# A two-layer graph attention kernel: adjacency requests and layer-1 pieces in other places of the issue order

## The chip, the cores and the metric

The kernel runs on one core of one Trainium2 chip. The metric is the device time of one execution in microseconds (us), lower is better. The kernel before was run three times: 2113.18, 2113.61 and 2120.83 us, with a median of 2113.61. One more execution was recorded by the profiler; it took 2115.05 us.

Names of engines: PE is TensorE, DVE is VectorE, ACT is ScalarE, POOL is GpSimd, SP is SyncE (here it only issues DMAs). L1029 is line 1029 of the kernel before.

## What is computed

There are 4096 nodes with 512 features (`x`) and a 4096 x 4096 symmetric 0/1 adjacency `adj`. Layer 0 is graph attention with 8 heads of width 64 over the whole adjacency, layer 1 is an attention inside 32 graphs of 128 consecutive nodes. Each layer adds its input and normalizes the rows.

```python
def layer0(X, A, W, a_self, a_neigh, b):          # 8 heads of 64
    feats = einsum('nf,hfo->hno', X, W)
    s_self = einsum('hno,ho->hn', feats, a_self)
    s_neigh = einsum('hno,ho->hn', feats, a_neigh)
    dense = s_self[:, :, None] + s_neigh[:, None, :]
    dense = where(dense > 0, dense, 0.2 * dense) * A[None]
    attn = softmax(dense, axis=-1)                 # not masked: non-neighbours count as exp(0)
    out = einsum('hij,hjo->hio', attn, feats) + b[:, None, :]
    return relu(out.transpose(1, 0, 2).reshape(N, 512))
def layer1(x, b, edge, ptr, Wq, bq, Wk, bk, Wv, bv):
    a = where(same_graph, (x @ Wq.T + bq) @ (x @ Wk.T + bk).T / sqrt(512), 0)
    s = (a + b + edge) * where(same_graph, 1, -1e6)
    return (softmax(s) * same_graph) @ (x @ Wv.T + bv)
x = layernorm(x + layer0(x, adj, ...))
return layernorm(x + layer1(x, adj, adj, ...))
```

## The kernel before

**Layer 0** goes over the adjacency in 4 passes r = 0 to 3, one for each pair of heads (`main_pass`, L1263). A pass has 4 chunks c of 1024 destination nodes, and a chunk has 32 row blocks j of 128 source nodes. These are taken in cycles of 8 (`wide=8`, passes 0 to 2) or 4 (pass 3). For a cycle the code writes out: the DMA loads of scaled features (f_s, g_s); for each j and head a tile q on DVE (L1310, 128 x 1024: the larger of a row p_row and a scalar, times the transposed adjacency tile `at`) and its 0/1 mark on ACT (L1319) or DVE (L1315); the matmuls accf (L1330, from `at`); the matmuls acc (L1347, from q); every 8 blocks the matmuls dens (L1361, from the marks).

**A^T tiles.** `bring` (L1074) makes the tile `at` for a step (r, c, j). In pass 0 it takes adjacency rows in fp8 (`a_b`, asked for by `load_adjacency`, L569, on POOL's DMA queue, which converts from fp32; 3 buffers), transposes them on PE (L1088), copies them to fp32 on ACT (L1092) and also writes them to DRAM as at_d (L1093, POOL's queue). In later passes it loads at_d on SP's queue (L1078). A cycle brings the tiles of the next one; the list `follow` (L1299) says which. There are 6 buffers of `at`, and 6 more in passes 0 to 2.

**Set-up** (L578 to L793) goes over 8 blocks k of 512 nodes. A block loads x rows (SP), transposes them (`turn_rows`, L635), computes scores on PE (L644) which ACT copies to st (L652), the exponentials from st (PE L658, then ACT and DVE), and features of four tiles u (L715). `scaled_features` scales a tile on DVE (gst, L729, 2 buffers) and on ACT and DVE (fst, L737 and L738, 2 buffers) and writes both to DRAM as g_d (256 KB) and f_d (512 KB) on POOL's queue (L750). The rows of exponentials go to DRAM as pu_d (L702) and, turned, into pu_all by a copy on DVE (L708). After the last block, S_col is made on DVE from 32 small matmuls (L785 to L793). Three adjacency requests, for row blocks 0, 4 and 8 of chunk 0, stand in the set-up at the ends of blocks 4, 5 and 6 (L778). Two rows p_row of 512 KB (broadcast from pu_d), for the first chunk, are loaded on SP's queue.

**End of a chunk.** `sums_to_rows` (L1127) adds accf and acc to ys and copies dens to dcs; its pieces, the item E below, transpose dcs (L1178, 4 times) and ys (L1201, 8 times) on PE, reduce the counts on DVE (`parts` L1181, `rd` L1191 to L1194) and scale ys to hst (L1202). In pass 3 the result and the earlier heads (hp_l, loaded from DRAM) are joined to x1b (L1123, 8 operations for a block of 512 rows) and normalized: statistics L524 and L525 on DVE, rstd on POOL (L527, L528), the result on DVE (L530).

**Layer 1** goes over 8 blocks of 512 nodes. A block is a generator (`layer_1`, L931) whose pieces are: transposes of x1b (L937, two pieces), zT (L957, then ACT's copy L964, two pieces), then scores in one piece (L984, the minimum on DVE L993, the exponentials ns on ACT L1009, `values(0)` L1029, transposes of ns L1058 with ACT's copy pT_f L1060, `values(1)`), `rows_out((0, 1))` (L1043, y_f on DVE L1045, layer norm, output), `values(2)` and `values(3)`, `rows_out((2, 3))`. `values` is four L1029 matmuls and one addition v_t on DVE (L1037).

**The order of the work.** PE's instructions run in the order in which the code writes them out. In pass 3, from chunk 1 on, pieces of E and of layer 1 are woven into layer 0's cycles by a written plan: `PLAN` (L1235) has for each cycle of four row blocks (group) two strings; the first is run ahead of the cycle's acc matmuls and the second behind them (`pieces`, L1276, called at L1340 and L1358). A letter advances a generator by one piece: E the chunk's end, b and a two blocks of layer 1, R the join of a second block. What is left after pass 3 is run by one last string (L1428), the tail. The other engines' instructions are put in order by a scheduler; each engine and each DMA queue keeps its order. PE's small results go to PSUM tiles from `misc` (L548), which takes its pools in turn; after pass 0 these hold three buffers (ps_misc 1, ps_misc2 2).

Of the kernel before, what the change touches and what calls it, by code (L numbers as in the profile page):

```python
# [404 lines left out]
def adjacency_streamed_path(  # L405
# [32 lines left out]
    NT = N // P  # L438
    FC = F // P
    PR = H // 2  # L440
# [6 lines left out]
    NCH = N // C  # L447
# [100 lines left out]
    def misc(shape, dtype=F32):  # L548

        banks.append(banks.pop(0))  # L550
        return banks[-1].tile(shape, dtype, name="ps_m")
# [4 lines left out]
    def ring(name, pool, n):  # L556

        if name not in more:
            return pool
        k = turns[name] % (n + more[name][1])  # L560
        turns[name] += 1
        return pool if k < n else more[name][0]
# [6 lines left out]
    def load_adjacency(c, j):  # L569

        a_b = pools["adj"].tile([P, CT, 4 * P], FP8, name="a_b8")
        a_bs[c, j] = a_b
        return nc.gpsimd.dma_start(
            a_b, adj[ts(c, C), j * P : (j + 4) * P].rearrange("(t p) n -> p t n", p=P)
        )


    with tc.tile_pool(name="setup1", bufs=1, side="right") as one, tc.tile_pool(  # L578
# [11 lines left out]
        def load_rows(k):  # L590
            xts[k] = []
            for u in range(4):
                xt = xtp.tile([P, F], F32, name="xt_f")
                nc.sync.dma_start(xt, x[ts(4 * k + u, P), :])
                xts[k].append(xt)
# [34 lines left out]
        def turn_rows(k):  # L630
            xT = xTs[k] = two.tile([P, FC, 4, P], F32, name="xT_f")
            for c in range(FC):
                pt = pss.tile([P, 4, P], F32, name="ps_set")
                for u in range(4):
                    nc.tensor.transpose(pt[:, u, :], xts[k][u][:, ts(c, P)], ident)  # L635
                nc.scalar.activation(
                    xT[:, c], pt, AF.Identity, accum_out=xs[:, c, k : k + 1]
                )

        def scores(k):  # L640

            ps = pss.tile([P, 4 * P], F32, name="ps_set")
            for c in range(FC):
                nc.tensor.matmul(  # L644
                    ps[32 * c : 32 * c + 32, :],
                    wa[:, c, :],
                    xTs[k][:, c].rearrange("p u n -> p (u n)"),
                    start=True,
                    stop=True,
                )  # L650
            st = sts[k] = one.tile([P, 4 * P], F32, name="st")
            nc.scalar.copy(st, ps)  # L652
# [51 lines left out]
        def columns_of_exponentials(k):  # L704
            pc = pss.tile([P, 4, 2 * H], F32, name="ps_set")
            for u in range(4):
                nc.tensor.transpose(pc[:, u, :], rows[k][:, ts(u, P)], ident[: 2 * H, : 2 * H])
            nc.vector.tensor_copy(  # L708
                pu_all[:, 4 * k : 4 * k + 4].rearrange("p u k h -> p u (k h)"), pc
            )  # L710

        def features(k, u):
            pf = pss.tile([P, H * FH], F32, name="ps_set")
            for c in range(FC):
                nc.tensor.matmul(  # L715
                    pf,
                    tile_j(xTs[k][:, c].rearrange("p u n -> p (u n)"), u),
                    w_sb[:, c, :],
                    start=(c == 0),
                    stop=(c == FC - 1),  # L720
                )
            fb = three.tile([P, H, FH], F32, name="fb")
            nc.vector.tensor_add(fb.rearrange("p h o -> p (h o)"), pf, b_row)
            return fb

        def scaled_features(k, u, fb):
            j = 4 * k + u
            gst = two.tile([P, PR, 2, FH], F32, name="gst")
            nc.vector.tensor_tensor(  # L729
                gst.rearrange("p r h o -> p (r h) o"),  # L730
                fb,
                e_all[:, j, 1, :, None].to_broadcast([P, H, FH]),
                OP.mult,
            )
            fst = two.tile([P, PR, 2, FP], F32R, name="fst")
            fr = fb.rearrange("p (r h) o -> p r (h o)", h=2)
            nc.scalar.activation(fst[:, :, 0, :], fr, AF.Copy, scale=-1.0)  # L737
            nc.vector.scalar_tensor_tensor(  # L738
                fst[:, :, 1, :],
                fr,  # L740
                -1.0,
                fst[:, :, 0, :].bitcast(F32),
                op0=OP.mult,
                op1=OP.subtract,
            )
            for dst, n, src in (
                (g_d, FP, gst.rearrange("p r h o -> p r (h o)")),
                (f_d, 2 * FP, fst.rearrange("p r s n -> p r (s n)").bitcast(F32)),
            ):
                nc.gpsimd.dma_start(dst[:, k, :, ts(u, n)].rearrange("r p n -> p r n"), src)  # L750

        turn_rows(0)
        for k in range(NB):
            if k + 1 < NB:
                load_rows(k + 1)
            fbs = [features(k, 0)]
            if k == 0:
                fbs.append(features(k, 1))
                scores(0)
            else:  # L760
                exponentials(k)
            if k + 1 < NB:
                turn_rows(k + 1)
            if k == 0:
                exponentials(0)
            scaled_features(k, 0, fbs[0])
            if k:
                fbs.append(features(k, 1))
                columns_of_exponentials(k - 1)
            scaled_features(k, 1, fbs[1])  # L770
            fbs.append(features(k, 2))
            scaled_features(k, 2, fbs[2])
            if k + 1 < NB:
                scores(k + 1)
            rows_of_exponentials(k)
            fbs.append(features(k, 3))
            scaled_features(k, 3, fbs[3])
            if k in (4, 5, 6):  # L778
                tc.keep_in_program_order(load_adjacency(0, 4 * (k - 4)))
        xsum = one.tile([P, FC], F32, name="xsum")  # L780
        nc.vector.tensor_reduce(xsum, xs, AX.X, OP.add)
        pS = pss.tile([P, PR], F32, name="ps_set")
# [291 lines left out]
    def bring(r, c, j):  # L1074

        if r:
            at = ats[r, c, j] = ring("at", atp, 6).tile([P, C], F32R, name="at")
            nc.sync.dma_start(at.bitcast(F32), at_d[c, j])  # L1078
            return
        if j % 2:  # L1080
            return
        if j % 4 == 0 and (c, j) not in a_bs:
            load_adjacency(c, j)
        pairs = a_bs[c, j - j % 4].rearrange("p t n -> p (t n)").bitcast(BF16)
        pairs = pairs.rearrange("p (t k n) -> p t k n", t=CT, k=2)[:, :, j % 4 // 2, :]
        pt = misc([P, CT, P], BF16)
        for t in range(CT):
            nc.tensor.transpose(pt[:, t, :], pairs[:, t, :], ident_b)  # L1088
        both = pt.rearrange("p t n -> p (t n)").bitcast(FP8).rearrange("p (n k) -> p n k", k=2)
        for k in range(2):  # L1090
            at = ats[r, c, j + k] = ring("at", atp, 6).tile([P, C], F32R, name="at")
            nc.scalar.copy(at, both[:, :, k])  # L1092
            nc.gpsimd.dma_start(at_d[c, j + k], at.bitcast(F32))  # L1093
# [138 lines left out]

    PLAN = [("bE", ""), ("bb", ""), ("b", "a"), ("Ra", "a"), ("a", "b"), ("ba", "b")]  # L1235
    PLANS = PLAN + [("ab", ""), ("aaba", "")], PLAN + [("a", ""), ("aa", "a")]
    plan = {"b": None}

    def run_plan(todo):
        for k in todo:  # L1240
            gen = ends[0] if k == "E" else plan[k]
            if gen is not None:
                next(gen)
            if k == "E":
                ends.pop(0)
# [15 lines left out]
    steps = [(r, c, j) for r in range(PR) for c in range(NCH) for j in range(NT)]  # L1261

    def main_pass(r, ae=None, wide=4):  # L1263

        for c in range(NCH):
# [19 lines left out]
            for j0 in range(0, NT, wide):  # L1285
# [10 lines left out]
                if at_step == 0:  # L1296
# [2 lines left out]
                follow = [  # L1299
                    x  # L1300
                    for x in steps[at_step + wide : at_step + 2 * wide]
                    if x[0] == r or 0 < r < x[0] and (x[0] < PR - 1 or x[2] < 4)
                ]
                qs = {}
                for j in cycle:
# [99 lines left out]
        banks.remove(psx)  # L1405
    first_pass.close()
    banks.extend([ctx.enter_context(tc.tile_pool(name="ps_misc2", bufs=2, space=PSUM))] * 2)
    for x_ in steps[NT * NCH : NT * NCH + 8]:
        bring(*x_)
    with tc.tile_pool(name="wl1", bufs=1, side="right") as wp:  # L1410
        work.append(weights_of_layer_1(keep, wp))
        work.append(kind_of_graphs(wp))
# [2 lines left out]
        for gen in work:  # L1415
            for _ in gen:
                pass
        work.clear()
    main_pass(2, wide=8)
    more.clear()  # L1420
    wide_passes.close()
    with tc.tile_pool(name="lp", bufs=2) as lp, tc.tile_pool(
        name="lp1", bufs=1
    ) as lp1, tc.tile_pool(name="lp2", bufs=2) as lp2:
        pools.update(lp=lp, lp1=lp1, lp2=lp2)
        main_pass(3)
        plan["K"] = kind_of_inputs(lp1)
        run_plan("bEbbbbbaaRaaKKbbababaababbbb")  # L1428


@with_exitstack
# [50 lines left out]
```

## Time and profile before

| what | value |
| --- | --- |
| median of 3 runs | 2113.61 us |
| the profiled execution | 2115.05 us |
| span of its instructions | 2113.0 us |
| mean granted TensorE clock | 0.989 of full speed |
| PE busy | 2059.4 us (97%) |
| DVE busy | 1660.3 us (79%) |
| ACT busy | 1533.8 us (73%) |
| POOL busy | 243.1 us (12%) |
| q, L1310 on DVE | 1024 of 1278 ns |
| acc, L1347 on PE | 8192, 902.7 us |
| accf, L1330 on PE | 2048, 495.3 us |

The span runs from the first to the last instruction, and the execution's time is 2.05 us longer. Busy time of an engine is the time in which one of its instructions runs; loads of weights run beside the matmuls and are listed apart. Lines of a timeline give start, duration, engine, line, operation, its operands, how often it comes in a row, and in brackets the idle time before it with what ended it.

### The profile page before, as it was taken

The page shows a single profiled execution, that of the slowest core. Times are in us where ns is not written, and L with a number is a line of the kernel's source. Part 1 is how long each engine was busy: PE and PEld are TensorE (multiplying, and loading weights), DVE is VectorE, ACT ScalarE, POOL GpSimd, SP SyncE. Part 2 cuts the span into 40 slices and gives each one's busy share as a digit, 9 for nine tenths or more (in the row PEclk, how much of TensorE's full clock was granted, in tenths as well). Part 3 has the DMA queues.
Part 4 walks back from the last instruction along what each step waited for, and adds up shares of the span by engine and source line. Part 5 has one row for each costly group of instructions (what it writes and reads, how often), then busy time and mean ns, then how long its engine had stood idle before and what let it go on. Part 6 is the DMA issues. An engine that isn't in the chain of part 4 may idle for free. (4 is left out here: it accounts for less than half of the span.)

```text
span 2113.0 us, 38133 instructions
## 1 busy us (share of the span) xinstructions
PE 2059.4 (97%) x15012; PEld 1016.1 (48%) x15012; DVE 1660.3 (79%) x2032; ACT 1533.8 (73%) x1818; POOL 243.1 (12%) x391
## 2 busy tenths in 40 slices
PE   8998999999999999999999999999999999999997
PEld 4545555455545444445445444544444445445443
DVE  5556887878789998787999999999974884786744
ACT  3327898888868889787889989998884567468320
POOL 2343222222100000000000000000210110210110
PEclk9998999999999999999999999999999999999999
DMA  8999999999879999887999999989964674665211
GB/s 246 278 215 249 276 290 258 296 256 296 267 270 342 326 366 357 273 311 254 330 319 339 306 349 325 327 304 351 307 210 144 225 250 158 207 239 165 70 48 42
DMA packets 207881, 551.28 MB, mean 261 GB/s; under 512 B 25292, under 2 KB 66252, under 8 KB 207692
## 3 DMA queue, kind: packets, MB, share of 16 engines
q1 hardware_dynamic: 140748, 425.79, 58.0%
q0 software_dynamic: 62784, 121.91, 23.0%
q8 instruction: 120, 1.97, 0.4%
q10 hardware_dynamic: 4160, 1.05, 0.2%
q14 instruction: 69, 0.57, 0.1%
HBM read 491.79 MB, written 107.22 MB: 283 GB/s over the span
## 5 line engine op out<-in xcount | busy, mean ns | idle before, releaser
L1310 DVE SCALAR_TENSOR_TENSOR q<-p_row,d_all,at 128x1024 f32<-128x1024 f32 x1024 | 1242.1, 1278 | 181.4 <-PE acc L1347 147.9
L1319 ACT ACTIVATE mark<-q,nb_all 128x1024 fp8e4<-128x1024 f32 x896 | 993.2, 1144 | 217.6 <-DVE q L1310 202.0
L1347 PE MATMUL acc<-q,g_s 128*32 128x512 f32 x8192 | 902.7, 594 | 2.9 <-DVE q L1310 2.5
L1347 PEld LDWEIGHTS acc<-q,g_s 128*32 128x32 f32 x8192 | 264.9, 110 | 594.8 <-issue 534.0
L1330 PE MATMUL accf<-at,f_s 128*128 128x512 f32 x2048 | 495.3, 398 | 5.1 <-DMA at<-at_d 4.3
L1330 PEld LDWEIGHTS accf<-at,f_s 128*128 128x128 f32 x2048 | 380.7, 189 | 115.5 <-issue 25.9
L1107 ACT ACTIVATE ck<-ck,neg_half_f 128x1024 f32<-128x1024 f32 x128 | 145.9, 1140 | 21.8 <-DMA ck<-in_adj_dram 21.5
L1108 ACT ACTIVATE ck<-ck,neg_quarter 128x1024 f32<-128x1024 f32 x128 | 146.3, 1143 | 1.9
L1092 ACT CAST at<-ps_m 128x1024 fp32r<-128x1024 fp8e4 x128 | 120.1, 1023 | 10.8 <-issue 5.9
L1029 PE MATMUL ps_m<-wvT,x1T 128*128 128x512 f32 x256 | 119.3, 615 | 6.8 <-DVE y_f L1045 6.8
L1361 PE MATMUL dens<-mark,e_b 128*6 128x512 fp8e4 x2048 | 124.3, 379 | 0.7 <-ACT mark L1319 0.7
L715 PE MATMUL ps_set<-w_sb_f,xT_f 128*128 128x512 f32 x256 | 115.4, 599 | 0.0
L957 PE MATMUL ps_m<-x1T,M_sb 128*128 128x512 f32 x256 | 113.1, 596 | 1.2 <-ACT x1T L938 1.2
L1212 POOL DMA_DIRECT2D hs_d<-hst x12 | 10.7, 895 | 847.4 <-DVE hst L1202 753.4
L1315 DVE TENSOR_SCALAR mark<-q,d_all 128x1024 fp8e4<-128x1024 f32 x128 | 95.8, 749 | 4.8
L737 ACT ACTIVATE fst<-fb 128x512 fp32r<-128x512 f32 x32 | 20.3, 634 | 101.0 <-DMA f_d<-fst 80.4
L1361 PEld LDWEIGHTS <-e_b 128*6 128x6 bf16 x2048 | 52.8, 86 | 79.8 <-issue 36.6
L1093 POOL DMA_DIRECT2D at_d<-at x128 | 69.4, 542 | 172.4 <-ACT at L1092 105.0
L1029 PEld LDWEIGHTS ps_m<-wvT,x1T 128*128 128x128 f32 x256 | 49.8, 198 | 65.4 <-issue 55.1
L957 PEld LDWEIGHTS ps_m<-x1T,M_sb 128*128 128x128 f32 x256 | 48.0, 190 | 62.6 <-issue 59.2
L1037 DVE TENSOR_TENSOR v_t<-ps_m,bv_row 128x512 f32<-128x512 f32 x32 | 21.9, 684 | 69.4 <-PE ps_m L1029 69.4
L715 PEld LDWEIGHTS ps_set<-w_sb_f,xT_f 128*128 128x128 f32 x256 | 48.8, 198 | 49.0 <-issue 48.7
(172 smaller groups left out, 1128.4 us busy)
## 6 DMA issues: line engine op xcount, KB each, us to landing
at<-at_d SPq DMA_DIRECT2D x384, 512.0 KB, 6.3
ck<-in_adj_dram SPq DMA_DIRECT2D x128, 512.0 KB, 5.5
f_s<-f_d SPq DMA_DIRECT2D x128, 512.0 KB, 7.3
at_d<-at POOLq DMA_DIRECT2D x128, 512.0 KB, 14.9
g_s<-g_d SPq DMA_DIRECT2D x128, 256.0 KB, 5.8
f_d<-fst POOLq DMA_DIRECT2D x32, 512.0 KB, 7.3
p_row<-pu_d SPq DMA_DIRECT2D x32, 512.0 KB, 7.4
a_b<-in_adj_dram POOLq DMA_DIRECT2D x32, 512.0 KB, 16.3
```

The source lines that it names most:

```text
L715: nc.tensor.matmul(pf, tile_j(xTs[k][:, c].rearrange("p u n -> p (u n)"), u), w_sb[:, c, :], start=(c == 0), stop=(c == FC - 1),)
L957: nc.tensor.matmul(pz, L1["M"][:, f, ts(c, P)], x1T[:, f, :], start=(f == 0), stop=(f == FC - 1),)
L1029: nc.tensor.matmul(pv, x1T[:, f, ts(u, P)], L1["wvT"][:, f, :], start=(f == 0), stop=(f == FC - 1),)
L1092: nc.scalar.copy(at, both[:, :, k])
L1107: tc.keep_in_program_order(nc.scalar.activation(ck, ck, AF.Square, bias=neg_half))
L1108: nc.scalar.activation(ck, ck, AF.Abs, bias=neg_quarter, accum_out=binp[:, k : k + 1])
L1310: nc.vector.scalar_tensor_tensor(q, p_row[h], d_j, ats[r, c, j].bitcast(F32), op0=OP.max, op1=OP.mult)
L1315: nc.vector.tensor_scalar(mark, q, d_j, None, op0=OP.is_gt, saturate=False)
L1319: nc.scalar.activation(mark, q, AF.Sigmoid, bias=nb_all[:, j, hh : hh + 1], scale=BIG, saturate=False,)
L1330: nc.tensor.matmul(accf[:, s, :], f_s[j // 4][:, j % 4, w, :], ats[r, c, j][:, ts(s, HB)], start=(j == 0 and w == 0), stop=(j == NT - 1 an ...
L1347: nc.tensor.matmul(acc[o : o + 32, s, :], g_s[j // 4][:, j % 4, h, o % FH : o % FH + 32], qs[j, h][:, ts(s, HB)], start=(j == 0), stop=(j ...
L1361: nc.tensor.matmul(dens[lo : lo + 6, :], e_b[:, j, 2 * r + h, :], marks[j, h][:, ts(s, HB)], start=(j == 0), stop=(j == NT - 1),)
```

## The change

It has three parts.

1. The transposed tiles for the first cycle of pass 1 (8 loads on SP's queue) are asked for in the last cycle of pass 0 by `follow`, and no more by a loop of their own between the two passes.
2. The three adjacency requests of the set-up stand at the ends of blocks 3, 4 and 5, no more of blocks 4, 5 and 6.
3. In pass 3, the first two groups of a chunk's plan are ("E", "b") and ("b", "b"), no more ("bE", "") and ("bb", ""). So E is ahead of the acc matmuls of group 0 as before, one piece of layer 1 moves from ahead of E to behind acc, and of group 1's two pieces one moves behind acc. In the tail the first three letters are bbE, no more bEb.

```diff
-            if k in (4, 5, 6):
-                tc.keep_in_program_order(load_adjacency(0, 4 * (k - 4)))
+            if k in (3, 4, 5):
+                tc.keep_in_program_order(load_adjacency(0, 4 * (k - 3)))
...
-    PLAN = [("bE", ""), ("bb", ""), ("b", "a"), ("Ra", "a"), ("a", "b"), ("ba", "b")]
+    PLAN = [("E", "b"), ("b", "b"), ("b", "a"), ("Ra", "a"), ("a", "b"), ("ba", "b")]
     PLANS = PLAN + [("ab", ""), ("aaba", "")], PLAN + [("a", ""), ("aa", "a")]
...
                 follow = [
                     x
                     for x in steps[at_step + wide : at_step + 2 * wide]
-                    if x[0] == r or 0 < r < x[0] and (x[0] < PR - 1 or x[2] < 4)
+                    if x[0] == r or x[0] < PR - 1 or x[2] < 4
                 ]
...
     banks.extend([ctx.enter_context(tc.tile_pool(name="ps_misc2", bufs=2, space=PSUM))] * 2)
-    for x_ in steps[NT * NCH : NT * NCH + 8]:
-        bring(*x_)
...
-        run_plan("bEbbbbbaaRaaKKbbababaababbbb")
+        run_plan("bbEbbbbaaRaaKKbbababaababbbb")
```

## The prediction

> **What bounds the kernel now.** I read the page's busy shares and slices first.
>
> ```profile
> PE 2059.4 (97%) x15012; PEld 1016.1 (48%) x15012; DVE 1660.3 (79%) x2032; ACT 1533.8 (73%) x1818; POOL 243.1 (12%) x391
> ...
> PEclk9998999999999999999999999999999999999999
> ```
>
> The reader is to see that PE runs 97% of the span at nearly full clock. The change takes no matmul away, so it can win only idle time of PE (53.6 us in all) and the time matmuls lose to a halved clock. So second I listed what PE waited for.
>
> ```profile
> PE ps_m L1029 <- DVE y_f L1045: 6.8, 2, 3.4
> PE ps_m L1088 <- DVE pu_all L708: 4.9, 1, 4.9
> PE accf L1330 <- DMA at<-at_d: 4.3, 2, 3.8
> PE ps_m L1058 <- ACT ns L1009: 4.1, 1, 4.1
> PE ps_m L1201 <- DVE v_t L1037: 4.0, 2, 2.1
> ```
>
> Total, number and longest wait stand at the end of each line. Five rows, 24.1 us, are the places the change is near: chunk starts in pass 3 (L1029, L1201: chunks 2 and 3), the end of set-up (L1088), the boundary of passes 0 and 1 (L1330), the tail (L1058). Third, PE's timeline around chunk 3's start:
>
> ```profile
> 1828.66 0.60 PE L1201 MATMUL ps_m<-ident_f,ys 128*128 128x128 f32 x4
> 1831.41 1.02 PE L1201 MATMUL ps_m<-ident_f,ys 128*128 128x128 f32 x4 [2.15 <-DVE v_t L1037]
> 1832.37 8.34 PE L1347 MATMUL acc<-q,g_s 128*32 128x512 f32 x64
> ...
> 1853.12 6.54 PE L1029 MATMUL ps_m<-wvT,x1T 128*128 128x512 f32 x8 [3.41 <-DVE y_f L1045]
> ```
>
> The gap is not the whole loss: eight L1029 matmuls take 6.54 us here, 3.60 elsewhere, and the acc set 8.34, not 7.07. The table by windows gives the reason (after PE's, PEld's, DVE's, ACT's and POOL's busy time comes PEclk); the first line is the same step one chunk earlier:
>
> ```profile
> 1645.00:1660.00 15.00, 13.17 (x72) 6.30 (x74) 10.94 (x21) 10.10 (x16) 2.07 (x2) 1.00 0.87 314
> 1829.00:1838.00 9.00, 6.85 (x51) 2.15 (x53) 6.48 (x14) 1.00 (x1) 0.00 (x0) 0.81 0.35 109
> ```
>
> **What the Trainium skill says.** "TensorE: Matmul & The Clock Gate", section "What's actually happening": the clock falls to half after an idle window of some 3.4 us, counted by a free-running window; section "Part 4: PE-mode transpose": transposes don't count as busy as matmuls do. The trace agrees: gaps of 1.83 and 3.41 us at chunk 2 leave the clock at 1.00; gaps of 2.15 (transposes just before) and 3.41 at chunk 3 halve it. "DMA: Bandwidth & Descriptors", section "Queues, rings and completion order": each DMA engine serves its queue rows in turn, packet by packet, so one queue's order is kept while another proceeds. Here a g_d write lands in about 3 us when nothing is ahead, and in 12.6 us (153.47 to 166.04) behind an a_b request.
>
> **Edit 1, A^T loads for pass 1 in the last cycle of pass 0: 0 us.** The built order of before already has these eight SP loads where the edit writes them; between set-up and pass 3 the two programs hold the same instructions with the same waits on every engine. The 3.82 us wait stays.
>
> **Edit 2, adjacency requested one block earlier.** The requests stand on POOL's DMA queue between the g_d and f_d writes (set-up end, from the timeline of all engines):
>
> ```profile
> 152.58 0.92 POOL L573 DMA_DIRECT2D a_b<-in_adj_dram  x1
> 153.47 0.78 POOL L750 DMA_DIRECT2D g_d<-gst  x1
> ...
> 166.13 0.69 DVE L729 TENSOR_TENSOR gst<-fb,e_all 128x512 f32<-128x512 f32 x1 [5.28 <-DMA g_d<-gst]
> 167.38 0.63 ACT L737 ACTIVATE fst<-fb 128x512 fp32r<-128x512 f32 x1 [7.35 <-DMA f_d<-fst]
> ...
> 170.75 0.22 DVE L708 COPY pu_all<-ps_set 128x64 f32<-128x64 f32 x1
> 171.02 1.22 PE L1088 MATMUL ps_m<-ident_b,a_b 128*128 128x128 bf16 x9 [4.94 <-DVE pu_all L708]
> ```
>
> a_b holds block 7's writes up, gst and fst (two buffers each) wait for them, S_col and L708 stand behind on DVE, PE behind L708. Without a_b there, gst is free at about 160, fst at about 164 (a write after it without it lands in 3 to 5 us); S_col still waits for PE's x sums (165.1), so L708 comes at about 167 and PE goes on at 167.3: gain 3.7. Cost: block 4's writes are now behind an a_b requested at about 93.75, just when two p_row broadcasts (512 KB each, 93.6 to 103.1) and the x rows of block 6 move. f_d of block 4's first tile landed at 107.16; a_b takes 9.5 us beside x rows, 5.9 alone, so it lands at 110 to 114. PE's L658 waits for ACT's st copy (L652), queued behind an fst; before, the copy ended 3.0 us before PE needed it (107.80 + 0.57 against 111.43). So a stall of 0 to 4, I take 3; block 5's a_b adds some 1.9 at block 6's L658, because those had no slack (stalls 0.11 and 0.24 before, which go). Total cost 1.9 to 6, I take 4.5. Net +0.8, from -2.5 to +4, one half-clock window included.
>
> **Edit 3, other places.** In chunk 1 no layer-1 block is open, so nothing moves. At chunks 2 and 3, group 0 has E's 12 transposes (3 x 0.60) first, then acc, then values and pT (L1029 x8, L1058, L1029 x8); group 1 has L1043 before acc and L1029 x16 after it. Nothing is removed: only waits change. The two waits of before go: E's second half waited for a PSUM buffer behind v_t, which sits behind x1b on DVE; now all three buffers are free at 1645.7. L1029 no longer waits for y_f with acc queued behind it. What comes late next, by walking DVE's queue with its rows (q 1.28, parts and rd 1.1, hst 0.685, x1b 0.55, y_f 0.744, v_t 0.684): q of row block 3 queues behind E's parts, rd, hst and x1b, and acc waits 0.65 and 0.8; values waits 1.1 for the buffer that the second hst frees at 1660.6; in group 1, q behind two y_f costs acc 0.5 and 0.8. Sum 3.85 against 1.83 + 3.41 = 5.24: gain 1.4 in chunk 2. Chunk 3 lost more: from the first acc of the chunk to its first dens of group 1, chunk 2 takes 1686.47 - 1633.21 = 53.26 us, chunk 3 1866.48 - 1808.43 = 58.05. The 4.8 are 0.32 of longer gap and the half clock (acc 1.27, L1029 2.9, transposes 0.36). Split into waits of about 1 us between matmuls, the clock should hold, so chunk 3 wins 1.4 + 4.8 = 6.2. Below: nothing if DVE is the bound, and only the clock is saved (4.5); above: both gaps and the clock, 5.2 + 10.0 = 15.
>
> Tail: L984 now precedes E, so ns and its exponentials (L1009) are ready before L1058. Gone: 4.11 idle and the half clock after it,
>
> ```profile
> 2006.71 1.63 PE L1058 MATMUL ps_m<-ident_f,ns 128*128 128x128 f32 x4 [4.11 <-ACT ns L1009]
> 2008.13 5.76 PE L1029 MATMUL ps_m<-wvT,x1T 128*128 128x512 f32 x8
> ```
>
> which cost 1.03 in L1058, 2.16 in L1029 and 0.2 in L1043: 7.5 in all. New: L984 waits about 0.75 for zT on ACT (one copy is 0.69), E's second half 0.4 for the buffer that L993 empties, and the second L1043 about 2.6 for v_t, which DVE has behind the four L530 that wait for POOL's rstd (1.09 there before); 0.7 for half clock after it. Sum 4.45; gain 3.1 (1 to 6).
>
> **Sum.** 0 + 0.8 - 1.4 - 6.2 - 3.1 = -9.9. The profiled execution took 2115.05 us (span 2113.0 and 2.05 around it) and the median is 2113.61; the stalls sit in the same places whichever is taken, so I subtract from the median: 2103.7, said as 2104. The measurement can tell about 0.5% from no change, 10.6 us: faster means below 2103.0, slower above 2124.2.
>
> **Rivals.**
> (B) Software writes get their turn beside the broadcasts, since the queues are served in turn: then block 4 stalls nothing and only 1.9 remains, edit 2 gives 1.9 - 3.7 = -1.8, and about 1 more from a spared half-clock window; with edit 3's -10.7 that is -13.5: 2100. For it: round-robin service. Against it: between 98 and 101.5 the software queue moved nothing while p_row did.
> (C) DVE becomes the bound at chunk starts: E's DVE work (parts and rd 1.1, two hst 1.3, eight x1b 3.2, four stats with their aggregates 3.3, four L530 1.9) comes to 10.8 us, and is now ahead of q's; DVE is at 10.94 of 15 us in the window shown, so it has 4.1 to spare. Gains at chunk 2 vanish, chunk 3 wins its 4.8 at most, and the tail gives 1; with edit 2 at +2.5 that is -3.3: 2110. For it: 79% busy DVE and its strict queue. Against it: E's work is the same amount as before, done at the same chunk starts.
> (D) Slower: the early a_b collides with block 6's x rows. They landed at 105.1 to 110.5, and PE's transposes L635 need them at 112.28. If a_b delays them by its own 6 us they land at 116.5 and PE stops 4.2 us, with two half-clock windows (3.4); with 4.5 of queue waits and the gain of 3.7 that is +8.4, and chunk starts give only the 4 of the clock: 2118. It decides once the last x row lands after 112.3. Against it: they are on another queue, and have 1.8 us of slack.
> (E) The chunk starts keep no wait worth naming (15.2), the tail gives 3.1 and edit 2 costs nothing: -18.3, 2095.
> That the change doesn't do what it says is certain for edit 1 and in the forecast at nought.
>
> **Chances.** Forecast 0.46 (own range 2100 to 2108), B 0.20, C 0.20, D 0.09, E 0.05. Under 2103.0 lie four tenths of the forecast, nearly all of B, and E: 0.42. Over 2124.2 only the far end of D and what I haven't thought of: 0.05. The rest, 0.53. The range leaves out E and most of D, some 0.15 in all, and takes in the bounds of edits 2 and 3 that the cases use: 2096 to 2114.
>
> **What would show it.** Right: L1088 after set-up waits about 1.2 us, not 4.94; L658 of block 5 shows a wait of about 3 on st; no L1201 wait at chunks 2 and 3, PEclk 1.00 at both; chunk 3's stretch from first acc to the first dens of group 1 about 52 us; the tail's L1058 without wait; the 3.82 at the pass boundary unchanged. Wrong: L635 waiting for xt_f in set-up beyond the waits of before (D), acc waiting for q by more than 2 us at chunk starts (C), or no new wait at L658 (B).

## The result, and the profile after

| | before | after |
| --- | --- | --- |
| median of 8 runs each | 2116.70 us (2113.10 to 2123.19) | 2104.86 us (2102.94 to 2108.87) |
| ratio after / before, 95% interval | | 0.995 (0.9936 to 0.9964) |
| profiled execution | 2115.05 us | 2104.88 us |
| span | 2113.0 us | 2102.9 us |
| mean granted TensorE clock | 0.989 | 0.992 |

The ratio is 10.6 us on 2116.7, with an interval from 7.6 to 13.5; the medians differ by 11.84. The two profiled executions differ by 10.17 us. Here is the list of what PE waited for in the kernel after, the answer to the list of before:

```profile
PE ps_set L658 <- ACT st L652: 3.9, 2, 3.7
PE accf L1330 <- DMA at<-at_d: 3.9, 2, 2.9
...
PE ps_m L1043 <- DVE v_t L1037: 1.8, 1, 1.8
...
PE ps_m L1088 <- DVE pu_all L708: 0.7, 1, 0.7
```

The reader is to see that three rows of before are gone (L1029 for y_f, L1201 for v_t, L1058 for ns, 14.9 us together), that L1088's wait fell from 4.9 to 0.7, that L658, 0.2 us before, now has 3.7 us at one place, and that one row is new: L1043, 1.8 us. PE's timeline around chunk 3's start shows the first group as it is now:

```profile
1823.10 1.04 PE L1201 MATMUL ps_m<-ident_f,ys 128*128 128x128 f32 x8
1824.07 5.36 PE L1347 MATMUL acc<-q,g_s 128*32 128x512 f32 x48
1829.64 3.10 PE L1347 MATMUL acc<-q,g_s 128*32 128x512 f32 x16 [0.22 <-DVE q L1310]
...
1853.56 7.13 PE L1029 MATMUL ps_m<-wvT,x1T 128*128 128x512 f32 x16
```

E's eight transposes run in one piece. The 64 acc matmuls took 8.34 us before because of the clock; here the first 48 take 5.36 us at full clock, and the last 16 take 3.10 in place of 1.77: they wait for q in small bits. The sixteen L1029 run without a gap. The table by windows has PEclk at 1.00 from 1829 to 1838, where before had 0.81 (the work in this window is a little further on now):

```profile
1829.00:1838.00 9.00, 8.64 (x36) 3.18 (x33) 8.62 (x19) 2.30 (x3) 1.38 (x2) 1.00 0.60 194
```

From 1515 to 2090 us PEclk is 1.00 throughout in the kernel after.

Where the 10.2 us are, by landmarks read off the two traces: accf starts after set-up 2.15 us later (177.01 against 174.86); passes 0 to 2 and the beginning of pass 3 take 2.40 us longer; chunk 2's start (first acc to the first dens of group 1, as the prediction has it) is 2.81 shorter and chunk 3's 7.60 shorter; the tail, from the last dens to PE's last matmul, is 4.37 shorter. The stretches between are equal within 0.02. Sum: -10.23. What the prediction calls the first acc of a chunk is the last acc set of the chunk before: in PE's order it stands ahead of the chunk's first accf and of E. The stretch holds the same matmuls in all kernels, so the comparison is not touched by the name.

### The profile page after: what moved, and what is told of

Its sections match the earlier page's. It is cut to its first block, busy times and chain, and to the rows that moved or that the text cites. A ratio compares the mean times of both kernels' runs of the same rounds, so it can differ in the third digit from the quotient of the medians.

```text
span 2102.9 us, 38131 instructions
## 1 busy us (share of the span) xinstructions
PE 2061.3 (98%) x15012; PEld 1015.0 (48%) x15012; DVE 1659.0 (79%) x2032; ACT 1535.7 (73%) x1818; POOL 249.4 (12%) x391
## 5 line engine op out<-in xcount | busy, mean ns | idle before, releaser
L1330 PE MATMUL accf<-at,f_s 128*128 128x512 f32 x2048 | 494.4, 397 | 5.5 <-DMA at<-at_d 3.9
L1330 PEld LDWEIGHTS accf<-at,f_s 128*128 128x128 f32 x2048 | 378.7, 188 | 116.0 <-issue 25.6
L1029 PE MATMUL ps_m<-wvT,x1T 128*128 128x512 f32 x256 | 114.2, 594 | 0.0
L737 ACT ACTIVATE fst<-fb 128x512 fp32r<-128x512 f32 x32 | 20.3, 633 | 101.5 <-DMA f_d<-fst 76.8
L1029 PEld LDWEIGHTS ps_m<-wvT,x1T 128*128 128x128 f32 x256 | 47.6, 190 | 57.2 <-issue 56.0
```

What stands on the lines that cost most here:

```text
L1029: nc.tensor.matmul(pv, x1T[:, f, ts(u, P)], L1["wvT"][:, f, :], start=(f == 0), stop=(f == FC - 1),)
L1330: nc.tensor.matmul(accf[:, s, :], f_s[j // 4][:, j % 4, w, :], ats[r, c, j][:, ts(s, HB)], start=(j == 0 and w == 0), stop=(j == NT - 1 an ...
```

## The experiments

All landmarks in one table, in us, each from one profiled execution. "accf" is the start of the first L1330, "passes" the time from there to the start of the stretch of chunk 2 in pass 3, "chunk 2" and "chunk 3" the stretches named above, "tail" as above.

| kernel | accf | passes | chunk 2 | chunk 3 | tail |
| --- | --- | --- | --- | --- | --- |
| before | 174.86 | 1458.35 | 53.26 | 58.05 | 113.50 |
| after | 177.01 | 1460.75 | 50.45 | 50.45 | 109.13 |
| first_cycle_alone | 179.31 | 1460.41 | 54.10 | 54.16 | 113.70 |
| requests_alone | 178.26 | 1458.18 | 56.81 | 57.88 | 114.44 |
| places_alone | 177.12 | 1456.57 | 50.47 | 50.48 | 109.73 |
| first_request_block_0 | 176.52 | 1456.99 | 50.47 | 50.46 | 109.19 |
| places_group0_alone | 177.61 | 1458.70 | 49.16 | 49.14 | 112.85 |
| places_group1_alone | 177.58 | 1460.51 | 55.12 | 55.19 | 113.41 |
| tail_alone | 174.60 | 1457.88 | 54.70 | 53.12 | 108.66 |
| places_and_three_buffers | 168.62 | 1461.35 | 50.47 | 50.46 | 109.40 |
| change_and_three_buffers | 169.25 | 1461.70 | 50.47 | 50.47 | 109.33 |
| group0_tail_three_buffers | 170.14 | 1460.21 | 49.15 | 49.13 | 108.85 |
| E_then_b_ahead | 169.78 | 1457.61 | 51.13 | 51.49 | 109.23 |

Three things to read first. "Passes" wanders by 5 us (1456.57 to 1461.70) over kernels whose passes 0 to 2 hold the same instructions, and it does not go with any of the edits; so the 2.40 us that the kernel after shows there can't be put down to an edit. (All of the wander is in passes 0 and 1; pass 2 takes 371.94 us in all thirteen.) And accf in kernels with the set-up of before lies anywhere from 174.60 to 179.31. A profiled execution need not be a typical one: that of places_group1_alone was the slowest of its 22 runs, that of tail_alone the fastest of its 22.

**Edit 1 alone.**

```diff
-                    if x[0] == r or 0 < r < x[0] and (x[0] < PR - 1 or x[2] < 4)
+                    if x[0] == r or x[0] < PR - 1 or x[2] < 4
...
-    for x_ in steps[NT * NCH : NT * NCH + 8]:
-        bring(*x_)
```

> Edit 1 alone. Theory: 0 us, since the built order of the loads does not change; the wait of accf for at at the pass boundary stays within 1 us of 3.8 us, and the time within 2 us of the kernel before. Rival (the loads come earlier by some queue effect that the order does not show, as the 2.87 us of the changed kernel against 3.82 us might suggest): wait of 2.9 us or less in this run too, and 1 to 3 us faster.

Measured: ratio 1.0006 (0.9993 to 1.002). The wait of accf for at was 3.91 us. In tail_alone, which doesn't have edit 1, it was 2.90. So the 2.9 us of the kernel after is one of the values that this wait takes anyway. Edit 1 is worth nothing that the runs show; the rival falls.

**Edit 2 alone.**

```diff
-            if k in (4, 5, 6):
-                tc.keep_in_program_order(load_adjacency(0, 4 * (k - 4)))
+            if k in (3, 4, 5):
+                tc.keep_in_program_order(load_adjacency(0, 4 * (k - 3)))
```

> Edit 2 alone, the rest as before. Theory: a new wait of 3 to 4 us at PE's L658 in block 5 (for st), with the clock at half for two windows behind it, so the transposes of block 6 start 6 to 7 us later than before; 4 to 5 us of it come back where set-up ends (L1088 waits under 1.2 us instead of 4.94), so accf starts 1.5 to 2.2 us later than before, and the time is 1 to 5 us over before. Rival (the net loss in the changed kernel was a chance of that run): accf starts no later than before and the time is 0 to 2 us under it.

Measured: ratio 1.0017 (1.0007 to 1.0027), which is 3.6 us slower (1.5 to 5.7). PE waits 3.67 us at L658, with the clock at half from 114.43 for two windows, and L1088's wait for pu_all is 0.2. How the wait comes about is in the timeline of all engines of the kernel after, which has the same set-up:

```profile
92.33 0.80 SPq L1269 DMA_DIRECT2D p_row<-pu_d  x2
...
93.18 0.91 POOL L573 DMA_DIRECT2D a_b<-in_adj_dram  x1
...
113.59 0.63 ACT L737 ACTIVATE fst<-fb 128x512 fp32r<-128x512 f32 x1 [9.82 <-DMA f_d<-fst]
114.13 0.57 ACT L652 COPY st<-ps_set 128x512 f32<-128x512 f32 x1
...
114.75 1.89 PE L658 MATMUL ps_set<-stack,st 128*128 128x16 f32 x8 [3.70 <-ACT st L652]
```

The reader is to follow it upwards: PE waits for ACT's copy st, the copy stands on ACT behind an fst, the fst waits 9.82 us for a buffer that an f_d write still reads, and that write was behind the a_b request, issued 0.85 us after the two p_row broadcasts. This a_b landed 17.3 us after its issue, at 110.4; the three of before took 12.2 to 13.7. Some of the delay is older than a_b: the f_d write ahead of it, beside the broadcasts, took 10.6 us and landed at 103.0.

**Edit 3 alone.**

```diff
-    PLAN = [("bE", ""), ("bb", ""), ("b", "a"), ...
+    PLAN = [("E", "b"), ("b", "b"), ("b", "a"), ...
...
-        run_plan("bEbbbbbaa...
+        run_plan("bbEbbbbaa...
```

> Edit 3 alone, set-up as before. Theory: the chunk starts and the tail give all of it: from first acc to the first dens of group 1 about 50.5 us in chunks 2 and 3 (53.3 and 58.1 before), the tail about 4.9 us shorter, together 13 to 16 us under before, which is 3 to 5 us faster than the whole change. Rival (part of the gain at the chunk starts comes from where the clock's windows fall, which edit 2 shifts): 8 to 11 us under before, no faster than the whole change.

Measured: ratio 0.9946 (0.9925 to 0.9967), 11.4 us on 2118.1 with an interval from 7.0 to 15.9; the medians differ by 14.9. By stages it is the theory's picture, 50.5 us at both chunk starts. The timing alone can't tell the theory's 13 to 16 us from the rival's 8 to 11, nor edit 3 alone from the whole change; the stretches, which do not depend on the set-up's phase any more (50.45 to 50.48 in five kernels), speak for the theory.

**The first request in block 0.**

```diff
-            if k in (3, 4, 5):
-                tc.keep_in_program_order(load_adjacency(0, 4 * (k - 3)))
+            if k in (0, 4, 5):
+                tc.keep_in_program_order(load_adjacency(0, 4 * max(k - 3, 0)))
```

> The whole change, but the first of the three adjacency requests stands at the end of set-up block 0 and not 3; the others stay at 4 and 5. Theory (the request in block 3 costs because it meets the two broadcast rows and x rows): the wait at L658 of block 5 falls from 3.7 us to under 1, set-up ends about 5 us earlier than in the changed kernel, and the time is 14 to 18 us under before. Rival (any third request overfills the software queue, and the wait only moves to another block): a wait of 2 to 4 us at L658 of an earlier block, and 8 to 12 us under before.

Measured against before: ratio 0.9945 (0.9925 to 0.9966). The wait at L658 of block 5 is gone, and one of 2.12 us stands at L658 of block 2, with a half-clock window behind it; accf starts at 176.52, no earlier to speak of than in the kernel after. The theory that only the broadcasts make the request dear fails: on this point the rival is right, the wait moved. The time, 11.6 us under before, is in the rival's range too. There, too, an fst waited, 11.07 us, for its f_d write.

**Only group 0 of the plan.**

```diff
-    PLAN = [("bE", ""), ("bb", ""), ...
+    PLAN = [("E", "b"), ("bb", ""), ...
```

> Of edit 3 only the first group of the plan: ("E", "b"), then ("bb", "") as before; set-up and tail as before. Theory (each group's place removes its own wait): the 1.1 to 2.4 us before L1201's second half go, about 1.5 us of waits within acc come; the 3.4 us wait of L1029 for y_f in group 1 stays, in most executions with the clock at half behind it. From first acc to the first dens of group 1 some 53 to 56 us at chunks 2 and 3, the time 2 to 6 us under before. Rival (E's work on DVE sets the pace of both groups): the second wait goes too or grows to 5 us; the stretch is 50.5 us or over 57.

Measured: ratio 0.9947 (0.9932 to 0.9962), 11.2 us faster, outside the 2 to 6 us expected. The theory fails; the rival is right that the second wait goes too, though it had the stretch at 50.5 us or over. PE's timeline of this run:

```profile
1655.78 3.11 PE L1347 MATMUL acc<-q,g_s 128*32 128x512 f32 x16 [0.22 <-DVE q L1310]
...
1671.62 7.03 PE L1029 MATMUL ps_m<-wvT,x1T 128*128 128x512 f32 x16
1678.58 7.07 PE L1347 MATMUL acc<-q,g_s 128*32 128x512 f32 x64
```

Group 1 has its old order (L1029 x16 ahead of acc), and the wait for y_f is gone all the same: sixteen L1029 in 7.03 us, then acc without a wait. The stretch is 49.15 us, 1.3 less than with both groups changed.

**Only group 1 of the plan.**

```diff
-    PLAN = [("bE", ""), ("bb", ""), ...
+    PLAN = [("bE", ""), ("b", "b"), ...
```

> Of edit 3 only the second group of the plan: ("b", "b"), with ("bE", "") ahead of it as before; set-up and tail as before. Theory: the 1 to 2.4 us before L1201's second half stay, the 3.4 us before L1029 go with the half clock behind them, and about 1 us of waits within acc comes: stretch 51 to 54 us at chunks 2 and 3, the time 4 to 9 us under before. Rival (DVE's work sets the pace): the wait moves to acc, 2 to 3 us of it, and the stretch is 54 us or over.

Measured: ratio 0.9986 (0.9977 to 0.9994), 3.0 us faster (1.3 to 4.9), at the lower end of the theory at best; the stretch of 55.1 us, from the slowest of the runs, is the rival's. PE's timeline of this run at chunk 2:

```profile
1660.85 1.02 PE L1201 MATMUL ps_m<-ident_f,ys 128*128 128x128 f32 x4 [1.93 <-DVE v_t L1037]
1661.79 8.35 PE L1347 MATMUL acc<-q,g_s 128*32 128x512 f32 x64
...
1675.64 1.92 PE L1347 MATMUL acc<-q,g_s 128*32 128x512 f32 x16
1678.32 7.89 PE L1347 MATMUL acc<-q,g_s 128*32 128x512 f32 x48 [0.75 <-DVE q L1310]
```

The wait at L1201 and the half clock after it are still there. In group 1 the 3.4 us before L1029 have become 0.75 before acc and 2.6 inside it (48 matmuls in 7.89 us, 5.3 undisturbed): the same wait at another place.

**Only the tail.**

```diff
-        run_plan("bEbbbbbaa...
+        run_plan("bbEbbbbaa...
```

> Of edit 3 only the tail (bbE in place of bEb). Theory: the 4 us wait of L1058 for ns and the half clock behind it go, a wait of 1.8 us of L1043 for v_t comes: from the last dens to PE's last instruction about 109.3 us in place of 113.5 to 114.4, so 3 to 6 us under before. Rival (the tail is bound by DVE's and POOL's chain of norms, and gains there are given back before the end): the stretch stays over 112 us, 0 to 2 us under before.

Measured: ratio 0.9985 (0.9975 to 0.9994), 3.2 us faster (1.3 to 5.3); the tail takes 108.66 us, L1058 doesn't wait, L1043 waits 1.84. The rival falls.

**Three buffers.** Two kernels, one with edit 3 alone and one with the whole change; gst and fst (and the set-up tile that shares fst's buffers) come from the pool with three buffers.

```diff
-            gst = two.tile([P, PR, 2, FH], F32, name="gst")
+            gst = three.tile([P, PR, 2, FH], F32, name="gst")
...
-            fst = two.tile([P, PR, 2, FP], F32R, name="fst")
+            fst = three.tile([P, PR, 2, FP], F32R, name="fst")
```

> Edit 3 alone, and three buffers for gst and fst in place of two; the requests stand at blocks 4, 5, 6 as before. Theory (two buffers are what lets a request for adjacency hold PE up): the waits at L658 go under 0.3 us, the wait of L1088 for pu_all falls from 4.2 to 5.1 us to under 1.5, accf starts at 171 to 174 us (174.9 to 179.3 without), and the time is 2 to 5 us under that of edit 3 alone. Rival (the software queue's own rate sets the end of set-up, whatever the buffers): L1088 still waits 3 us or more, the time equals that of edit 3 alone within 1.5 us.

> The whole change, and three buffers for gst and fst in place of two. Theory: the wait of 3.7 us at L658 in block 5 falls under 1 us, with no half clock behind it; accf starts at 170 to 173 us; the time is 3 to 7 us under that of the whole change. Rival (the broadcast rows hold the software queue up, and st waits whatever the buffers): the 3.7 us stay within 1 us.

Measured against before: 0.9907 (0.989 to 0.9924) with edit 3 alone, 0.9906 (0.9889 to 0.9923) with the whole change, medians 2096.26 and 2096.14 us, measured side by side. Neither lists a wait at L658, and in both L1088 waits 0.7. accf starts at 168.62 and 169.25, earlier than either expectation. So the buffers are what couples an adjacency request to PE, and with a third one the place of the requests makes no difference that the runs show. The gain over edit 3 alone, 8.5 us at accf and some 8 in the ratios, is more than the 2 to 5 us expected: not only L1088's wait goes but small ones ahead of it (0.39 and 0.82 at L658, 1.89 at L635 in places_alone), and the clock is at half for 6.83 us in place of 13.65.

**The parts that pay, together.**

```diff
-    PLAN = [("bE", ""), ("bb", ""), ...
+    PLAN = [("E", "b"), ("bb", ""), ...
...
-        run_plan("bEbbbbbaa...
+        run_plan("bbEbbbbaa...
```

with three buffers, as above.

> Group 0 of the plan and the tail as in the change, group 1 as before ("bb", ""), three buffers for gst and fst. Theory (group 1's new place only costs, once E is first): stretch 49.1 us at chunks 2 and 3 in place of 50.5, the time 2 to 4 us under edit 3 with three buffers, so 20 to 24 us under before. Rival (the 49.1 us hang on the set-up or tail of that run): 50.5 us again, and the time of edit 3 with three buffers within 1 us.

Measured: 2093.12 us median, ratio to before 0.9894 (0.9874 to 0.9914). By the ratios this is 2.7 us under places_and_three_buffers, though the intervals overlap. What settles it is the stretch, 49.15 and 49.13, as the theory has it: group 1's new place costs 1.3 us a chunk once E is first. The gain in time, 22.3 us on 2115.5, is in the expected 20 to 24.

**E first, the piece still ahead of acc.**

```diff
-    PLAN = [("E", "b"), ("bb", ""), ...
+    PLAN = [("Eb", ""), ("bb", ""), ...
```

(on group0_tail_three_buffers)

> As group0_tail_three_buffers, but group 0's strings are ("Eb", ""): E first, and the layer-1 piece still ahead of acc. Theory (both waits of before came from E's 10.8 us of DVE work starting late, and E's place alone is what cures them): L1029 does not wait for y_f, acc does not wait for q; the piece now waits 0 to 2 us for PSUM buffers of E; stretch 48 to 50 us, the time within 2 us of group0_tail_three_buffers. Rival (it is the piece's move behind acc that cures the second wait, by giving DVE 7 us more): the wait of L1029 for y_f of about 3 us is back, stretch 51 us or over, 3 to 8 us slower than group0_tail_three_buffers.

Measured: 2095.92 us, ratio to before 0.991 (0.9891 to 0.9929); the median is 2.8 us over group0_tail_three_buffers, not within the 2 us of the theory. PE's timeline at chunk 2:

```profile
1643.36 3.67 PE L1029 MATMUL ps_m<-wvT,x1T 128*128 128x512 f32 x8 [2.00 <-DVE parts L1181]
...
1664.67 7.03 PE L1029 MATMUL ps_m<-wvT,x1T 128*128 128x512 f32 x16
```

L1029 in group 1 has no wait for y_f, though the piece is ahead of acc again. So E's place alone cures it, as the theory says. The first y_f starts 38.6 us into the stretch (1665.97 - 1627.39), 3.4 earlier than in before, and is over at 39.3, when PE came to wait for it there; here PE comes 1.5 us later still. What the piece's move behind acc is worth is the 2.00 us that L1029 now waits for E's PSUM buffer (held until parts has read it). The stretch of 51.1 to 51.5 is longer than the 48 to 50 expected: at chunk 2 acc still waits for q inside (8.43 us for 64 matmuls, where the theory had no wait), and at chunk 3 the same 2.00 us of wait is followed by half clock (the eight L1029 take 5.37 us, not 3.67).

## Why the prediction was right, and where it was not

The forecast was 2104 us and 9.9 us less; 2104.86 and 10.6 less (7.6 to 13.5) were measured. That the absolute figure is met within 1 us is in part luck: the forecast was taken from the median of three runs of before, 2113.61, and eight runs gave 2116.70, from which the same gain leads to 2106.8. The gain holds as a sum, but two of its terms were off in opposite directions, and one argument was wrong.

**Edit 1, 0:** right, 1.0006 (0.9993 to 1.002).

**Edit 2, +0.8 net (-2.5 to +4):** the chain was found, not all of its sizes. f_d of block 4's first tile was to land at 110 to 114; the fst that waited for it ran at 113.59. The stall at L658 was put at 3 us and is 3.7; the next block's at 1.9, and there is none in the kernel after and 0.93 in requests_alone. L1088's gain was 3.7 and is 4.2. Undersized was the half clock: one window was allowed for, and there are two (from 114.76 for 6.83 us in the kernel after), which the kernel gets back at the end of set-up (half clock for 6.83 us there, 13.65 before). In these two profiles PE's last transposes of set-up (L707) come 6.36 us later, 171.42 against 165.06, where 4.5 was the cost taken, and 4.21 of it come back by accf. The net size stays open: the mean of accf is 177.6 in the two profiles with the new places and two buffers, 176.9 in the six with the old ones, +0.8, but those six alone spread over 4.7; the timing of edit 2 alone says +1.5 to +5.7. What the timing settles is that it gains nothing. Rival B, in which the software queue is served beside the broadcasts, falls with the stall of 3.7 us (its counter-argument was near the mark: in before, 15 of the 204 packets from 98 to 101.5 us were the software queue's, so it moved little, not nothing). Rival D fell too: block 6's x rows were no longer what PE waited for.

**Edit 3, -1.4, -6.2 and -3.1:** too small. At the chunk starts the mean stretch of the eight in the four kernels with the old plan is 55.3 us, the new one 50.5, so 9.6 us for both against 7.6 predicted. The walk along DVE's queue had 3.85 us of new waits in a chunk; 48.02 us would be left of chunk 2 without any wait, so 50.45 holds 2.4. Found as predicted: acc's last row block in group 0 (1.45 predicted; 0.2 ahead and 1.3 inside measured) and group 1's acc (1.3 predicted, 8.07 against 7.07 measured). Not found: the 1.1 us for values. The second hst does come late, at 1663.29, but the eight L1029 take 3.70 us where 3.60 is undisturbed. The sign set for rival C, acc waiting for q by more than 2 us, could not tell the two apart: the forecast's own walk has 2.75 us of it, and some 2.5 were measured. Rival E falls with the same 2.4 to 2.5 us of waits that are left in a chunk. The tail's new waits came to some 2.4 us and not 4.45: L984 0.4 (0.75 predicted), E's second half 0.15 (0.4), L1043 1.84 (2.6), and no half clock (0.7). That would make the gain 5.1. The mean tail is 109.2 us in the eight kernels with the new order and 113.6 in the five with the old one, 4.4 us; the 0.7 between is not accounted for.

That the sum came out right is therefore owed in part to offsets. By the landmarks, edit 3 brought 14.8 us in the two profiles; 2.15 went at set-up, within what set-up varies by, and 2.40 in passes 0 to 2, which can't be put down to an edit.

**The half clock at chunk 3** was booked as a fixed 4.8 us. It is not tied to chunk 3: requests_alone had it after both gaps of both chunks, first_cycle_alone and tail_alone after the second gap of each, and the stretch of the old plan ranges from 53.12 to 58.05. The trace of before was one draw of that. The new plan has it at neither chunk in any of its five kernels and always takes 50.5: its waits are short and scattered, and no 3.41 us window around them has under 2.0 us of busy PE. This agrees with the free-running window in the section "What's actually happening" of the Trainium skill's page "TensorE: Matmul & The Clock Gate", on which the step rested; the last section has the measured windows. They don't bear out two readings of the prediction: a window need not be idle for the clock to fall, and transposes are not shown to count less. In before, the gap of 1.83 us lay in a window with 1.61 us of busy PE, transposes included, and that of 2.15 in one with 1.26; the first kept the clock and the second did not.

**Wrong was the argument that each group's new place cures its own wait.** "L1029 no longer waits for y_f with acc queued behind it" took the y_f wait to be a matter of group 1's order. places_group0_alone and E_then_b_ahead show that it came from E being late: E stood behind the piece and its second half waited for a buffer besides, so the first hst started 1657.07 - 1633.21 = 23.9 us after the start of the stretch, against 1655.29 - 1637.76 = 17.5 us in the kernel after. With it came all that DVE has behind E: y_f started at 1675.15, 41.9 us into the stretch, and PE had come to it at 39.3; in the kernel after and in places_group0_alone it starts at 37.7. Rival C saw that DVE's order decides both groups, and drew the wrong conclusion: putting E's work ahead of q's doesn't make DVE the bound at these places, it takes the load off group 1. Of the two edits in the plan, the first brought everything and the second cost 1.3 us a chunk.

## What to carry to other kernels

When two waits lie close together, look for the work on the shared in-order engine that is late for both before giving each its own cure; try the cures one by one, since one of them may only cost. A write that waits in a DMA queue stops an engine through the number of its source buffers: count the buffers before moving the transfer that is ahead of it in the queue, because one more buffer can be worth more (8 us here) than any place for the transfer. And take a loss by the halved clock from one trace as a draw, not as a constant: whether a given gap halves the clock hangs on where the windows fall.

## What the runs showed of the hardware

**The clock is decided window by window.** In each of the thirteen traces the half-clock stretches start whole multiples of 3.413 us apart and, but for the last one, last 3.41, 6.83, 10.24 or 13.65 us; where this grid lies differs from trace to trace. So a gap can be weighed by the grid window that it falls in. In E_then_b_ahead the same wait of 2.00 us stands at chunks 2 and 3; these are the windows that end at 1643.11 and at 1817.19 (the first number after the length is PE's busy time):

```profile
1639.70:1643.11 3.41, 1.66 (x14) 1.32 (x12) 3.41 (x5) 3.32 (x4) 2.06 (x2) 1.00 1.02 404
1813.78:1817.19 3.41, 1.41 (x9) 0.92 (x8) 3.41 (x7) 3.32 (x3) 1.12 (x1) 1.00 0.93 311
```

With 1.66 us busy the clock stayed, with 1.41 it was halved from 1817.19. Counted over the 7787 windows of the thirteen traces that ran at full clock (from 20 us on, and with matmuls whose moving operand has one column left out), the clock fell 81 times: 79 times after at most 1.48 us of busy time, and after 1.60 and 1.92. Only two windows with less than 1.5 us, of 1.40 and 1.49, kept it. So in these traces a wait of 2 us is enough if it falls inside one window, and one of 3.4 us, split over two, may cost no clock: before, chunk 2.

**Transposes count towards busy time.** In before a window with 0.39 us of other matmuls and 2.2 us of transposes kept the clock (the clock does not fall at this place in any of the thirteen traces):

```profile
937.28:940.69 3.41, 2.61 (x23) 1.96 (x25) 1.90 (x6) 1.75 (x4) 0.89 (x1) 1.00 0.98 380
```

**Matmuls with one moving column hardly count.** At the end of set-up the clock fell with no gap ahead; here places_and_three_buffers:

```profile
160.00:164.00 4.00, 4.00 (x40) 3.84 (x41) 1.23 (x4) 0.63 (x1) 0.00 (x0) 1.00 0.76 285
164.00:168.00 4.00, 2.17 (x19) 1.84 (x18) 3.76 (x6) 3.96 (x5) 3.12 (x5) 0.51 0.63 204
```

From 160 to 164 PE is busy all the time, and yet the clock is at half from 164.07. What it did then were matmuls with a moving operand of one column (L785, to 163.1), then small transposes. L908 does the same in pass 1 of the kernel after, with neither a gap nor a transpose near:

```profile
965.13 4.12 PE L908 MATMUL ps_m<-b_q,w_k 128*128 128x1 f32 x32
```

The windows are those that end and begin where the clock falls:

```profile
964.68:968.09 3.41, 3.41 (x31) 3.33 (x29) 0.20 (x1) 0.00 (x0) 0.00 (x0) 1.00 1.02 370
968.09:974.92 6.83, 6.83 (x13) 3.53 (x14) 0.00 (x0) 0.17 (x1) 0.00 (x0) 0.50 0.32 127
```

The clock falls at this place in ten of the thirteen traces; in the other three, 1.49 to 1.56 us of other matmuls share the window. For most of it PE is loading weights (PEld, 3.33 of 3.41 us); whether that or the single column is what doesn't count, no run here separates.
